# The opening of a four-layer graph network on one core: load order, copies, and three jobs moved to GpSimd

## The chip, the cores and the metric

The kernel runs on one NeuronCore of a Trainium2 chip. The core has five instruction streams: TensorE (PE, with PEld for its weight loads), VectorE (DVE), ScalarE (ACT), GpSimd (POOL) and SyncE (SP). DMAs are issued from the streams of SP, ACT and POOL. The metric is the device time of the whole program in microseconds: 1605.96 before the change, the median of three runs (1605.39 to 1606.01).

## What is computed

Input `x` holds 32 graphs of 512 nodes with 128 features, in float32; `adj` is one 512 x 512 adjacency matrix for all of them. Four layers follow one another, each on a normalised and clipped input, and each added to `x`:

```python
h = maximum(layernorm(x), 0)
# layer 0: attention over edges
x_h  = elu(h @ Wi + bi)
e    = sigmoid(a_tgt[:, :, None] + a_src[:, None, :] + be) * mask   # mask = adj + 0.005 * (adj == 0)
agg  = einsum('bij,bjh->bih', e, x_h)
self_part = x_h * sum(e, axis=-1, keepdims=True)
x += concat([elu(concat([agg, self_part]) @ Wn + bn), x_h]) @ Wm + bm
# layer 1: five gated steps, each with adj @ h, then three gates; x += h
# layer 2: x += adj @ (h @ weight) + bias
# layer 3: x += sum over k of (adj^k @ h) @ W_k, k = 0..3, each power twice
```

The attention layer's "sum of the scores" is the sum of `e` over neighbours; it and the mask matter below.

## The kernel before, in words

One core handles the 32 graphs in eight groups of four (`G = 4`). A feature matrix is a tile of 128 partitions by 512 columns; the adjacency is four such tiles, here called quarters. All large products are on TensorE.

The program isn't written in its final order. Each step is recorded with `op(engine, cost, due, emit, reads, writes)`, and a planner (`Plan.order`, L135) lays the steps out engine by engine: it replays the recorded costs, starts on each engine the ready step with the earliest due time, and gives out buffers. The resulting order is fixed when the program is built; each engine then runs its own list in order, and semaphores hold an instruction until its inputs are there. `plan.nudge` (L233) shifts the due times of some steps by random amounts drawn from a list of seeds (`HEAD_NUDGES`, L25), for steps due between 0 and 130; the order up to 250 is laid out with them.

Where PE has no ready step the planner may put in `plan.idle` (L347), a product of the constant `ones` with itself that nothing reads. These are called fillers here. They are allowed until 50 on the planner's clock (`FILL`), and one is placed unless another PE step becomes ready within `idle.us` = 0.224.

The program opens as follows.
- SP loads graph 0 (`load_graph`, L377), weights and the next graphs. ACT issues the four quarters of the adjacency (L361 through `load`, called at L386) and then, with a first tiny `tanh` (L355), loads its function table. A hardware DMA's landing is told by one of eight semaphores that are handed out in turn, in program order; a ninth DMA waits, on the engine that issues it, until the first user of its semaphore has landed.
- PE turns the quarters (L574); ACT writes rounded copies of the quarters as they came (`nat`, L583) and of the turned ones (`adj_rows`, L584). DVE counts the entries that are neither 0 nor 1 (L560), PE adds the counts up (L590), and every engine reads the result and branches (L1106). With a binary adjacency the program goes to the arm `binary = True`, which runs in the profile.
- In the arm, 16 products of `nat` and `adj_rows` make the square of the adjacency (L906), the mask is made from `adj_rows` on ACT (L828), and the first four graphs go through the attention layer. `scored` projects a graph (L490 with `Wi_sb`), takes the ELU on ACT and DVE (L603 to L615), makes messages and end scores (L643). `aggregated` makes the four score tiles `es` on ACT (L704), masks them on DVE (L707), multiplies them with the messages (L715) and sums them for `self_part`.
- That sum is made in three ways: for graphs 0 and 1 the four tiles are added in two pairs on DVE (L727) and each pair is multiplied with `ones` on PE; for graph 2 the four are added into one by three additions on DVE (L736), split into a high and a low rounded part (L747, L748) and multiplied with `ones_r` (L753); from graph 3 on the additions are accumulating DMAs (L743).
- Layer norms put a power of -0.5 on POOL (L527) between DVE's moments (L522 to L525) and its scaling (L542).

Of the kernel before, what the change touches and what calls it, by code (L numbers as in the profile page):

```python
# [21 lines left out]


HEAD, TAIL = 250.0, 1500.0
HEAD_NUDGES = (7100000, 7100078, 7100153, 7100154, 7100740, 7100413, 7100768, 7100794, 7100559, 7100664, 7100595,  # L25
    7100631, 7100754, 7100963, 7100652, 7100659, 7100662, 7100678, 7100697, 7100699, 7100706,
    7100965, 7100730, 7100733, 7100742, 7100786, 7100966, 7100797, 7100813, 7100877, 7100824,
    7100834, 7100860, 7100864, 7100866, 7100875, 7100881, 7100884, 7100901, 7100907, 7100908,
    7100911, 7100919, 7100920, 7100922, 7100934, 7100936, 7100941, 7100945, 7100946, 7100949,
    7100950, 7100955, 7100970, 7100973)  # L30
TAIL_NUDGES = ()


# [19 lines left out]
class Plan:  # L53
# [7 lines left out]
    def __init__(self, slots, ahead, last):  # L61
        self.ahead, self.last, self.ops, self.vals = ahead, last, [], {}
        self.free = {k: [(0.0, i) for i in range(n)] for k, n in slots.items()}
        self.until = dict.fromkeys(self.RESULT, 0.0)
        self.shared, self.now = 0.0, 0.0
        self.careful = 0.0
        self.slack = 0.0
        self.pieces = {}
        self.cold = 4.5
        self.fill = 0.0  # L70
        self.idle = None
        self.complete = False

    def op(self, eng, us, due, emit, reads=(), writes=(), two=None, keep=0, result=None,
# [60 lines left out]
    def order(self, end=None):  # L135
# [35 lines left out]
        while events:  # L171
# [3 lines left out]
            for e in self.until:  # L175
                while coming[e] and coming[e][0][0] <= now:
                    _, i, o = heapq.heappop(coming[e])
                    heapq.heappush(ready[e], (o.turn, i, o))
                if self.until[e] > now:
                    continue  # L180
                passed, o = [], None
                while ready[e] and o is None:
                    x = heapq.heappop(ready[e])
                    if begins(x[2], now):
                        o = x[2]
                    else:
                        passed.append(x)
                for x in passed:
                    heapq.heappush(ready[e], x)
                if o is not None and now < self.careful and any(  # L190
                    c.turn < o.turn and t < now + 0.3 * o.us for t, _, c in coming[e]
                ):
                    heapq.heappush(ready[e], (o.turn, index[o], o))
                    o = None
                if o is None and e == "PE" and self.idle.known <= now < self.fill and not (
                    coming[e] and coming[e][0][0] < now + self.idle.us):
                    order.append(self.idle)
                    self.until[e] = now + self.idle.us * (1.9 if now < self.cold else 1.0)
                    heapq.heappush(events, self.until[e])
                if o is None:  # L200
                    continue
                order.append(o)
                o.begun = True
                while oldest + 1 < len(by_turn) and by_turn[oldest].begun:
                    oldest += 1
                o.start, self.until[e] = now, now + o.us
                if o.two:
                    self.shared = self.until[e]
                for v in o.takes:
                    v.slot = self.free[v.kind].pop(self.clean(now) if v.added else 0)[1]  # L210
                    if v.kind == "b":
                        self.pieces[v.slot] = v.pieces
                o.known = self.until[e] + o.result
                heapq.heappush(events, self.until[e])
                heapq.heappush(events, o.known)
                for v in o.vals:
                    v.left -= 1
                    if not v.left and v.kind:
                        self.free[v.kind].append((o.known, v.slot))
                        self.free[v.kind].sort()  # L220
                for a in o.after:
                    if a in index:
                        a.waits -= 1
                        a.ready = max(a.ready, self.known(o, a))
                        if not a.waits:
                            heapq.heappush(coming[a.eng], (a.ready, index[a], a))
                            heapq.heappush(events, a.ready)
# [24 lines left out]
def tile_four_graph_layers(  # L252
# [37 lines left out]
    MARGIN = 10.0  # L290
    FIRST = 4
    ONES = 0
    SPLIT = False
    SQUARE, NAT = 12.0, 0.0
    BRANCHES = 0.75
    A_LANDS = (3.0, 3.3, 3.6, 3.8)

    T_MM, T_TR, T_NARROW, T_PASS = 0.86, 0.44, 0.224, 0.23
    T_VEC, T_COPY, T_ACT, T_DMA = 0.605, 0.5, 0.6, 0.45
# [2 lines left out]
    plan = Plan(slots, ahead=60.0, last=(B - 2) * PACE)  # L302
    op = plan.op
    plan.careful = 18.0

    cpool = ctx.enter_context(tc.tile_pool(name="const", bufs=1))
    pool = ctx.enter_context(tc.tile_pool(name="slots", bufs=1))
# [28 lines left out]
    def chunks(t):  # L336
# [2 lines left out]

    ident, ones, neg_half = const("ident", [P, P]), const("ones", [P, P]), const("nhalf", [P, NC])  # L340
    op("POOL", 1.0, -9, lambda: make_identity(nc, at(ident)), [], [ident])
    op("DVE", 0.2, -9, lambda: nc.vector.memset(at(ones), 1.0), [], [ones])


    spare = places["b"].pop()
# [6 lines left out]
    op("POOL", 0.4, 5, lambda: nc.gpsimd.tensor_copy(at(ones_r), at(ones)), [ones], [ones_r])  # L352

    warm = Val("s")
    op("ACT", 1.4, -9, lambda: nc.scalar.activation(  # L355
        at(warm)[:, :1], at(ones)[:, :1], AF.Tanh), [ones], [warm])


# [15 lines left out]
        v.left += 1  # L374
    plan.vals.update(dict.fromkeys([*X_group, *X]))

    def load_graph(b, due, result=None):  # L377
        op("SP", 0.48, due, lambda: nc.sync.dma_start(
            at(X[b]), x[b].rearrange("(p c) d -> p c d", c=NC)),
            [], [X_group[b // G], X[b]] if b % G == 0 else [X[b]], result=result)  # L380


    load_graph(0, -10, 2.5)
    A_nat = [Val("f") for _ in range(NC)]
    for ic, v in enumerate(A_nat):
        load(v, adj.rearrange("(p c) n -> c p n", c=NC)[ic], -9.5, 0.45, result=A_LANDS[ic], eng="ACT")  # L386
    Wi_sb = load_const(Wi, [P, P], "Wi_sb", -9)
    bi_sb = load_column(bi, "bi_sb", -9)
    load_graph(1, -8.5, 4.3)
    load_graph(2, -8, 4.5)  # L390


    W_tok = const("W_tok", [P, P + 2])
    load(W_tok, Wn[:P], -7, to=lambda t: t[:, :P], result=4.5)
    load(W_tok, We.rearrange("(t p) o -> p (t o)", p=P), -7, to=lambda t: t[:, P:])
    be_sb = load_const(be.partition_broadcast(P), [P, 1], "be_sb", -7, result=4.3)
    Wn_sb = load_const(Wn[P:], [P, P], "Wn_sb", -6, result=4.0)
    bn_sb = load_column(bn, "bn_sb", -6, result=3.6)
    Wm_sb = load_const(Wm.rearrange("(t p) o -> p t o", p=P), [P, 2, P], "Wm_sb", -5)
    bm_bc = load_const(bm.partition_broadcast(P), [P, P], "bm_bc", -5, earliest=BRANCH)  # L400
    load_graph(3, -6, 3.6)

# [177 lines left out]
    plan.vals.update(dict.fromkeys([adj_r, *adj_rows]))  # L580
    nat = [Val("q") for _ in range(NC)]
    for jc, pt in enumerate(adjacency_turned(-1)):
        op("ACT", T_COPY, NAT + jc, lambda jc=jc: nc.scalar.copy(chunks(at(nat[jc])), by_token(A_nat[jc])), [A_nat[jc]], [nat[jc]])  # L583
        op("ACT", T_COPY, jc, lambda jc=jc, pt=pt: nc.scalar.copy(at(adj_rows[jc]), at(pt)),  # L584
           [pt], [adj_rows[jc], adj_r])
    p_odd = Val("b")
# [38 lines left out]
    def scored(b, hT, due):  # L625
        KEEP = 12
        if b >= G:
# [1 line left out]
        pace = 0.6 if b < FIRST else 1.0  # L629
        d = due + 6 * pace  # L630
        xhT = elu(product(Wi_sb, hT, d, blocks=b >= G), bi_sb, bi_half, d, KEEP,
                  relu_by_vector=b < 2)

        d = due + 14 * pace
        msg, ends = Val("f"), Val("s")
# [58 lines left out]
    def aggregated(b, begun, due):  # L694
# [28 lines left out]
        elif b < 2:  # L723
            ps = Val("b")
            pair = [Val("f"), Val("f")]
            for i in range(2):
                op("DVE", T_VEC, d - 6, lambda i=i: nc.vector.tensor_tensor(  # L727
                    at(pair[i]), at(es[2 * i]), at(es[2 * i + 1]), op=ALU.add),
                    [es[2 * i], es[2 * i + 1]], [pair[i]], two=True)
            for i in range(2):  # L730
                product(ones, pair[i], d - 1, ps, start=i == 0, stop=i == 1)
        else:
            sums = [Val("f")]
            if b < 3:
                for n in range(1, NC):
                    op("DVE", T_VEC, d - 10, lambda n=n: nc.vector.tensor_tensor(  # L736
                        at(sums[0]), at(es[0] if n == 1 else sums[0]), at(es[n]), op=ALU.add),
                        [es[n], es[0] if n == 1 else sums[0]], [sums[0]], two=True)
            else:
                op("SP", T_DMA, d - 10, lambda: nc.sync.dma_start(at(sums[0]), at(es[0])),  # L740
                   [es[0]], [sums[0]], result=2.6)
# [76 lines left out]
    def list_rest(binary, pool):  # L818
# [6 lines left out]
            rows = [Val(tile=adjT.tile[:, jc, :]) for jc in range(NC)]  # L825
        for jc, pt in enumerate([None] * NC if binary else adjacency_turned(9)):
            def masked(jc=jc):
                nc.scalar.activation(at(mask)[:, jc, :], at(adj_rows[jc]).bitcast(F32), AF.Identity,  # L828
                                     bias=at(ones)[:, :1], scale=1 / ALPHA - 1)
            if binary:  # L830
                op("ACT", T_COPY, 9 + jc, masked, [adj_rows[jc], ones], [mask])
                continue
            z, row = Val("f"), rows[jc]
            op("ACT", T_COPY, 9 + jc, lambda z=z, pt=pt: nc.scalar.mul(at(z), at(pt), 1 / ALPHA), [pt], [z])
# [66 lines left out]
        if binary:  # L901
            adj2T = Val(tile=pool.tile([P, NC, N], F32R, tag="AA", name="AA"))
            squares = [Val("b") for _ in range(NC)]
            for n in range(NC * NC):
                kc, jc = divmod(n, NC) if SPLIT else divmod(n, NC)[::-1]
                op("PE", T_PASS, SQUARE, lambda jc=jc, kc=kc, pt=squares[jc]: nc.tensor.matmul(  # L906
                    at(pt), at(nat[kc])[:, ts(jc, P)], at(rows[kc]), start=kc == 0, stop=kc == NC - 1),
                    [nat[kc], rows[kc]], [squares[jc]])
            for jc, pt in enumerate(squares):
                op("ACT", T_COPY, SQUARE, lambda jc=jc, pt=pt: nc.scalar.copy(  # L910
# [240 lines left out]
```

## Time and profile before

One execution was profiled. It took 1605.48 us by the device's clock; the profile's own span is 1603.6 us.

| engine | busy us | share | instructions |
|---|---|---|---|
| PEld | 1024.3 | 64% | 6321 |
| DVE | 1404.7 | 88% | 3314 |
| ACT | 1130.4 | 70% | 2129 |
| POOL | 240.3 | 15% | 240 |

The opening, in groups of instructions:

| line | engine, step | count | ns of one (mean; L707: median) |
|---|---|---|---|
| L583 | ACT, rounded copy of a quarter | 4 | 1147 |
| L828 | ACT, mask | 4 | 714 |
| L707 | DVE, masking of a score tile | 16 in the first 60 us | 682 |
| L527 | POOL, power | 128 | 1231 |
| L894 | POOL, folding weights, 64 columns | 6 | 1404 |

Times in the views are microseconds from the span's start. A row of the timeline gives the start, the length, the engine, the line, the operation, what it writes and reads, and in brackets how long the engine was idle before and what ended that. In a row of the windows the stretch is followed by the busy time of PE, PEld, DVE, ACT and POOL (with counts), the granted TensorE clock (1.00 is full), the share of the DMA engines that is busy, and GB/s. A float32 product stands in the records as two matmuls. Matmuls are pipelined, so the distance from one start to the next is what one costs, and the recorded length is longer.

### The profile page before, as it was taken

To read this page: it belongs to the slowest core of one execution; us is meant where nothing else is said; L and a number is where in the kernel's file an instruction comes from. 1 tells how busy PE (TensorE), PEld (TensorE's weight loads), DVE (VectorE), ACT (ScalarE), POOL (GpSimd) and SP (SyncE) were. 2 spreads that over 40 slices of the span, in tenths; PEclk is the share of its full clock that TensorE was granted. 3 is DMA by queue.
4 is the path that set the end of the run, shared out by engine and by line. 5 is a ranking of instruction groups with operands and counts; after the bars stand their busy time and mean duration, and the time that the engine had idled before them with its cause. 6 is when DMAs were issued, how large, how long until landed. Compare 5 with 4: busy or idle time off the path is not lost.

```text
span 1603.6 us, 20898 instructions
## 1 busy us (share of the span) xinstructions
PE 1596.1 (100%) x6321; PEld 1024.3 (64%) x6321; DVE 1404.7 (88%) x3314; ACT 1130.4 (70%) x2129; POOL 240.3 (15%) x240
## 2 busy tenths in 40 slices
PE   9999999999999999999999999999999999999998
PEld 7655555666666666666666666666666666656687
DVE  8899989998988899989988899888998889878862
ACT  8877777877866767667766678676787677665661
POOL 2121101211111111211111111111111101100010
PEclk9999999999999999999999999999999999999999
DMA  3365335443543345544445534454444444333221
GB/s 109 80 152 145 112 111 140 121 130 106 144 126 115 105 126 136 137 122 111 121 125 145 126 96 128 119 148 119 132 130 124 125 120 129 90 91 99 86 60 49
DMA packets 272634, 188.01 MB, mean 117 GB/s; under 512 B 77312, under 2 KB 221568, under 8 KB 272512
## 3 DMA queue, kind: packets, MB, share of 16 engines
q1 hardware_dynamic: 257824, 161.93, 33.8%
q0 software_dynamic: 12528, 22.81, 8.5%
q10 hardware_dynamic: 2160, 1.84, 0.3%
q8 instruction: 52, 0.85, 0.2%
q14 instruction: 70, 0.57, 0.1%
HBM read 82.78 MB, written 73.33 MB: 97 GB/s over the span
## 4 chain that ended last, share of the span: by engine, by line
PE 99%; DMA 0%; DVE 0%; ACTq 0%; issue 0%
PE b L490 46%; PE b L950 26%; PE b L1025 7%; PE b L715 7%; PE b L1034 4%; PE b L766 4%; PE b L643 2%; PE b L1013 2%; PE b L753 1%; DMA f<-in_adj_dram 0%; PE b L419 0%; PE b L347 0%; PE b L906 0%; ACTq L361 0%; PE b L680 0%; DVE s L522 0%
## 5 line engine op out<-in xcount | busy, mean ns | idle before, releaser
L479 ACT COPY f<-b 128x512 f32<-128x512 f32 x388 | 223.7, 584 | 146.5 <-PE b L950 101.1
L950 PE MATMUL b<-AQ,r 128*128 128x512 f32 x1024 | 305.4, 440 | 0.0
L527 POOL TENSOR_TENSOR s<-s,nhalf 128x4 f32<-128x4 f32 x128 | 156.6, 1231 | 968.2 <-DVE s L525 774.6
L950 PEld LDWEIGHTS b<-AQ,r 128*128 128x128 f32 x1024 | 192.3, 188 | 90.8 <-issue 50.0
L975 DVE TENSOR_TENSOR f<-f,b 128x512 f32<-128x512 f32 x320 | 212.7, 676 | 24.5 <-PE b L490 18.5
L431 DVE STREAM_TRANSPOSE f<-f 128x512 f32<-128x512 f32 x246 | 207.3, 846 | 20.7 <-ACT f L536 19.7
L536 ACT ACTIVATE f<-x,s 128x128 f32<-128x128 f32 x496 | 203.8, 487 | 27.7 <-DVE s L531 27.3
L950 PE MATMUL b<-adj_r,r 128*128 128x512 f32 x768 | 220.8, 430 | 0.0
L495 ACT ACTIVATE f<-f,b4w 128x512 f32<-128x512 f32 x160 | 115.6, 723 | 116.8 <-DVE f L975 116.3
L950 PEld LDWEIGHTS b<-adj_r,r 128*128 128x128 f32 x768 | 143.8, 188 | 59.2 <-issue 27.3
L924 DVE TENSOR_TENSOR r<-f,r 128x512 fp32r<-128x512 f32 x224 | 152.5, 683 | 13.1 <-ACT r L920 12.7
L490 PE MATMUL b<-f,w4T 128*128 128x512 f32 x320 | 163.2, 592 | 0.0
L490 PE MATMUL b<-f,u3T 128*128 128x512 f32 x320 | 163.1, 592 | 0.0
L490 PE MATMUL b<-f,w5T 128*128 128x512 f32 x320 | 162.9, 592 | 0.0
L490 PE MATMUL b<-f,u5T 128*128 128x512 f32 x320 | 162.9, 592 | 0.0
L490 PE MATMUL b<-f,w3T 128*128 128x512 f32 x320 | 162.7, 592 | 0.0
L495 ACT ACTIVATE f<-b,b5w 128x512 f32<-128x512 f32 x160 | 109.2, 684 | 54.9 <-PE b L490 49.9
L920 ACT CAST r<-f 128x512 fp32r<-128x512 f32 x224 | 137.7, 619 | 12.3 <-DMA f<-m 11.9
L495 ACT ACTIVATE f<-f,b3w 128x512 f32<-128x512 f32 x160 | 115.0, 721 | 38.9 <-DVE f L975 38.4
L992 DVE TENSOR_TENSOR f<-f,f 128x512 f32<-128x512 f32 x160 | 109.2, 683 | 30.7 <-ACT f L495 30.3
L1025 PEld LDWEIGHTS b<-V,f 128*128 128x128 f32 x1024 | 122.7, 192 | 14.8 <-issue 12.7
L743 POOL DMA_DIRECT2D f<-f x87 | 78.8, 918 | 348.9 <-DVE f L975 54.6
(114 smaller groups left out, 2370.4 us busy)
## 6 DMA issues: line engine op xcount, KB each, us to landing
m<-f SPq DMA_DIRECT2D x246, 256.0 KB, 2.1
f<-m SPq DMA_DIRECT2D x186, 256.0 KB, 2.9
f<-f POOLq DMA_DIRECT2D x87, 256.0 KB, 3.8
f<-m SPq DMA_DIRECT2D x240, 64.0 KB, 2.4
x<-in_x_dram SPq DMA_DIRECT2D x32, 256.0 KB, 3.1
f<-f SPq DMA_DIRECT2D x29, 256.0 KB, 2.4
f<-d SPq DMA_DIRECT2D x28, 256.0 KB, 5.5
out_dram<-x SPq DMA_DIRECT2D x28, 256.0 KB, 2.4
```

The lines of the kernel that those rows point to most:

```text
L431: op("DVE", us, due, lambda: nc.vector.transpose(view_out(at(blocks)), view_in(at(src))), [src], [blocks])
L479: op("ACT", us, due, lambda: nc.scalar.copy(at(t), at(src)), [src], [t])
L490: nc.tensor.matmul(to, at(w), of, start=start, stop=stop)
L495: op("ACT", us, due, lambda: nc.scalar.activation(at(dst), at(src), AF.Tanh, bias=at(bias), scale=scale), [src, bias], [dst])
L527: op("POOL", 1.2, due, lambda: nc.gpsimd.tensor_tensor(stat(SCALE), stat(VAR), at(neg_half), op=ALU.pow), [s, neg_half], [s], two=False)
L536: nc.scalar.activation(at(h)[:, ts(c, P)], at(X[b])[:, c, :], AF.Relu, bias=stat(SHIFT)[:, c : c + 1], scale=stat(SCALE)[:, c : c + 1],)
L715: op("PE", T_MM, d, lambda jc=jc: nc.tensor.matmul(at(pn), at(msg)[:, ts(jc, P)], at(es[jc]), start=jc == 0, stop=False), [msg, es[jc]], [pn])
L920: op("ACT", T_COPY, due, lambda: nc.scalar.copy(part(hi), whole()), [src], [hi], keep=1)
L924: op("DVE", T_VEC, due, lambda: nc.vector.tensor_tensor(part(lo), whole(), part(hi).bitcast(F32), op=ALU.subtract), [src, hi], [lo], two=two)
L950: nc.tensor.matmul(at(pa), at(part)[:, ts(jc, P)], view(at(columns)[:, jc, :]), start=jc == n == 0, stop=jc == NC - 1 and n == PARTS - 1,)
L975: op("DVE", T_VEC, d, lambda: nc.vector.tensor_tensor(at(s), at(u), at(pg), op=ALU.add), [u, pg], [s])
L1025: nc.tensor.matmul(at(pz)[:, ts(i, D)], at(t[i])[:, ts(ic, P)], at(V[k]), start=i == n == 0, stop=last and i == G - 1 and n == len(terms) - 1,
```

## The change

- Table load first: the tiny `tanh` gets an earlier due time than the adjacency loads, so ACT loads its table and then issues the quarters, and the quarters' loads are not to be planned before 1.0.
- The loads behind graph 0 get `earliest` times for the planner: graph 1 not before 2.6, five weight loads not before 3.5; expected landings are changed. In the built order SP issues graph 0, Wi, bi, graph 2, graph 3, bn, graph 1, and then the other weights. The fourth quarter's semaphore is then the one of bi.
- `nat` is written with the same column order as the quarter, not regrouped by `by_token`; the squares read it through `by_token` instead.
- The squares' order by output is fixed, and their due time is 9 instead of 12.
- The mask moves from ACT to GpSimd.
- The sums of the scores of graphs 0, 1 and 2 (four pair additions and three additions) move from DVE to GpSimd.
- Graph 2's relu, in the first ELU, moves from ACT to DVE (`relu_by_vector=b < 3`).
- Until 10 on the planner's clock a filler is placed only where no other PE step becomes ready within 0.7 (0.224 before, and still behind 10).
- A new list of seeds; since costs, engines and due times change too, the planned order differs everywhere.

The built program has 20 fillers instead of 34 in the arm that runs: 10 before the branch and 10 behind it, where there were 17 and 17.

```diff
-HEAD_NUDGES = (7100000, 7100078, 7100153, 7100154, 7100740, 7100413, 7100768, 7100794, 7100559, 7100664, 7100595,
...
+HEAD_NUDGES = (7500046, 7500070, 15001300, 7500191, 7500223, 15000120, 15000078, 15000080, 15000672, 15000178,
...
+        self.unsure = 0.0
...
-                    coming[e] and coming[e][0][0] < now + self.idle.us):
+                    coming[e] and coming[e][0][0] < now + (self.idle.us if now > self.unsure else 0.7)):
...
-    SPLIT = False
-    SQUARE, NAT = 12.0, 0.0
+    ADD = 1.15
+    SQUARE, NAT = 9.0, 0.0
...
-    A_LANDS = (3.0, 3.3, 3.6, 3.8)
+    A_LANDS = (2.15, 2.4, 2.65, 2.9)
...
+    plan.unsure = 10.0
...
-    op("ACT", 1.4, -9, lambda: nc.scalar.activation(
+    op("ACT", 1.4, -9.9, lambda: nc.scalar.activation(
         at(warm)[:, :1], at(ones)[:, :1], AF.Tanh), [ones], [warm])
...
-    load_graph(0, -10, 2.5)
+    load_graph(0, -10, 2.45)
...
-        load(v, adj.rearrange("(p c) n -> c p n", c=NC)[ic], -9.5, 0.45, result=A_LANDS[ic], eng="ACT")
+        load(v, adj.rearrange("(p c) n -> c p n", c=NC)[ic], -9.5, 0.45, earliest=1.0, result=A_LANDS[ic], eng="ACT")
...
-    load_graph(1, -8.5, 4.3)
-    load_graph(2, -8, 4.5)
+    load_graph(1, -8.5, 3.7, 2.6)
+    load_graph(2, -8, 3.9)
...
-        op("ACT", T_COPY, NAT + jc, lambda jc=jc: nc.scalar.copy(chunks(at(nat[jc])), by_token(A_nat[jc])), [A_nat[jc]], [nat[jc]])
+        op("ACT", T_COPY, NAT + jc, lambda jc=jc: nc.scalar.copy(at(nat[jc]), at(A_nat[jc])), [A_nat[jc]], [nat[jc]])
...
-                  relu_by_vector=b < 2)
+                  relu_by_vector=b < 3)
...
-                op("DVE", T_VEC, d - 6, lambda i=i: nc.vector.tensor_tensor(
+                op("POOL", ADD, d - 6, lambda i=i: nc.gpsimd.tensor_tensor(
                     at(pair[i]), at(es[2 * i]), at(es[2 * i + 1]), op=ALU.add),
-                    [es[2 * i], es[2 * i + 1]], [pair[i]], two=True)
+                    [es[2 * i], es[2 * i + 1]], [pair[i]], two=False)
...
-                    op("DVE", T_VEC, d - 10, lambda n=n: nc.vector.tensor_tensor(
+                    op("POOL", ADD, d - 10, lambda n=n: nc.gpsimd.tensor_tensor(
                         at(sums[0]), at(es[0] if n == 1 else sums[0]), at(es[n]), op=ALU.add),
...
-                nc.scalar.activation(at(mask)[:, jc, :], at(adj_rows[jc]).bitcast(F32), AF.Identity,
-                                     bias=at(ones)[:, :1], scale=1 / ALPHA - 1)
+                nc.gpsimd.tensor_scalar(at(mask)[:, jc, :], at(adj_rows[jc]).bitcast(F32), 1 / ALPHA - 1, 1.0,
+                                        op0=ALU.mult, op1=ALU.add)
...
-                kc, jc = divmod(n, NC) if SPLIT else divmod(n, NC)[::-1]
+                jc, kc = divmod(n, NC)
...
-                    at(pt), at(nat[kc])[:, ts(jc, P)], at(rows[kc]), start=kc == 0, stop=kc == NC - 1),
+                    at(pt), by_token(nat[kc])[:, jc, :], at(rows[kc]), start=kc == 0, stop=kc == NC - 1),
```

## The prediction

> **What bounds the kernel now.** I read the busy table first, then the chain of waits, then the windows by stage.
>
> ```profile
> PE 1596.1 (100%) x6321; PEld 1024.3 (64%) x6321; DVE 1404.7 (88%) x3314; ACT 1130.4 (70%) x2129; POOL 240.3 (15%) x240
> ...
> PE 99%; DMA 0%; DVE 0%; ACTq 0%; issue 0%
> ```
> ```profile
> 5.00:10.00 5.00, 4.39 (x37) 4.00 (x37) 4.53 (x20) 5.00 (x6) 2.23 (x4) 1.00 0.97 301
> 11.27:23.60 12.33, 12.15 (x72) 9.53 (x70) 10.54 (x40) 12.14 (x25) 4.83 (x9) 1.00 0.43 114
> 23.60:35.00 11.40, 11.38 (x60) 7.59 (x60) 11.23 (x40) 9.36 (x21) 2.51 (x2) 1.00 0.06 24
> 35.00:1550.00 1515.00, 1515.00 (x5817) 955.29 (x5816) 1359.66 (x3156) 1085.33 (x2043) 226.07 (x214) 1.00 0.44 120
> ```
>
> PE carries the chain, and from 35 us on it has no gap in 1515 us. So the time is a sum on PE: the moment real products start, plus real products, plus fillers behind that moment, plus PE's stalls. The change leaves the real products alone: I counted 4229 matmuls without fillers in both programs' orders. Only the head can move the time. A reordered step after 35 us costs nothing unless it opens a gap, and I find no step there whose inputs come later.
>
> What the head consists of, from the chain, the timeline of PE and that of ACT:
>
> ```profile
> 2.14 5.67 DMA f<-in_adj_dram
> ...
> 7.86 0.75 PE b L574 x4
> 8.60 1.12 PE b L347 x10
> 9.72 0.27 PE b L590 x8
> ```
> ```profile
> 4.87 4.32 ACT L583 CAST q<-f 128x512 fp32r<-128x512 f32 x4 [0.74 <-DMA f<-in_adj_dram]
> ...
> 9.08 2.04 ACT L584 CAST adj_r<-b 128x512 fp32r<-128x512 f32 x4
> ```
> ```profile
> 11.27 0.94 PE L906 MATMUL b<-adj_r,q 128*128 128x512 f32 x3
> ```
> ```profile
> 22.14 1.28 PE L347 MATMUL b<-ones 128*128 128x128 f32 x10
> 23.60 0.67 PE L715 MATMUL b<-f,f 128*128 128x512 f32 x1 [0.18 <-DVE f L707]
> ```
>
> The last adjacency quarter lands at 2.14 + 5.67 = 7.81, and the first square (L906) starts at 11.27. Behind that stand 17 fillers of two records each (L347: 2, 6, 10, 2, 2, 6 and 6 records); ten records lie 0.112 apart, so one filler is 0.224 us and all are 3.8 us. PE's bare stalls there are about 0.7: 0.35 ahead of 23.60 and 0.36 among the next three products.
>
> **Part by part.**
>
> *Adjacency behind the table load.* ACT's four adjacency issues go from 0.73 to behind table load and warm-up (1.28 + 0.20), to about 2.05, 2.5 and 3.0 (0.47 apart) for the first three. The fourth is worse off. Eight landing semaphores are handed out in turn; before, the ninth load (third graph) starts at 4.86, just after the first quarter landed. In the new order the fourth quarter is a reused one and waits for the column bi. Queued behind that wait on ACT are the rounded copies, whose inputs land later anyway. bi stands behind x0 and Wi (320 KB); POOL could use it at 6.33 before, and without adjacency beside it I estimate 4.7 to 5.2. More important, SP now issues the third and fourth graphs at 2.1 and 2.6 and the second one beside that fourth quarter. Before, x0, Wi, x1 and four quarters (1600 KB) were in by 7.81; now two graphs more (512 KB) stand ahead. The 5 to 10 us window shows the DMA engines 97% busy, in its full slices near 370 GB/s, so 512 KB are 1.4 us. As the graphs use another queue and may finish after the quarter, I take two thirds: landing at **8.7**, range 8.0 to 9.4.
>
> *Contiguous copies, fewer early fillers.* The four copies take 4.32 us, ending 9.19, behind the landing by 1.4. Contiguous, one costs what L584 costs a step, about 0.48, and only the last one is left behind the landing. Ready then are: transposes 0.75, four casts 3 x 0.48 + 0.61 (last row landing + 2.84, but the first square needs only early rows); the count: DVE's last L560 0.69, L542 1.03, L595 0.15, then 0.73 from L595's end to PE's branch, as now (10.17 to 10.90), so landing + 2.65. Before, ten fillers (1.12) also stood in front of the count. First square at landing + 2.75 instead of + 3.46: 8.7 + 2.75 = **11.45, +0.2 us**. The squares now load weights with a stride, as L574 does: its load is 0.06 longer than L419's, hidden below a pass of 0.23.
>
> *Fillers.* After the branch the new order has 10 instead of 17: 7 x 0.224 = **-1.6 us**, if no idle takes their place. Real PE work ahead of the first graph's product L715 in the new order: 16 squares 3.73, three projections 2.57, two turns 0.87, three weights 0.33, four swaps 0.93, four half-products 1.79, one spread 0.43, together 10.65; with 2.24 of fillers from 11.45 that is 24.3. DVE, resuming at 12.3, has 10.7 of rows (three moments 1.26, two norms 1.03, the ELU steps 0.60 to 0.65, small ones) plus one masking of 0.60: 23.6 to 24. They meet, so little idle replaces the fillers.
>
> *Mask to GpSimd.* ACT loses 4 x 0.61. GpSimd's price isn't in the trace; nearest are L352 and L932, 0.29 and 0.40 for 128 columns. With 0.21 as the fixed part (smallest L868) that makes 0.53 to 0.97; 1.6 at most if nothing is fixed. At 1.0, with two powers (1.03) in between, the masks end near 17.5, at 1.6 near 20. The first masking is at 23: nothing, cover 3 us. The second power and the swap cast wait behind them, each with over 1 us to spare. *Third graph's relu on DVE*: DVE +0.65, in the sum above.
>
> *Score sums to GpSimd.* Seven additions of 0.60 leave DVE. On GpSimd: folds L894 of 64 columns follow each other by 0.34, so 512 columns cost at most 2.7. [...]
>
> [...] The row first, POOL then DVE:
>
> ```profile
> 17.41 0.23 POOL L871 TENSOR_SCALAR b4w<-b4w 128x1 f32<-128x1 f32 x1
> ...
> 22.19 0.74 POOL L871 TENSOR_SCALAR b3w<-b3w 128x1 f32<-128x1 f32 x1
> ```
> ```profile
> 22.17 0.68 DVE L615 SCALAR_TENSOR_TENSOR f<-f,f 128x512 f32<-128x512 f32 x1
> ```
>
> The same tiny operation took 0.23 alone and 0.74 when it met L615, ending just behind it. Powers take 1.03 alone and 1.40 there; a fold 0.69 and 1.50. [...] In the trace GpSimd loses 0.4 to 0.8, while DVE beside the folds loses at most 0.23 (L924 0.92 for 0.69). [...]
>
> Who waits? Third graph: three additions in series after its last masking, 5.2, then cast 0.6, subtraction 0.7 and handoffs 0.2: ready at +6.7. PE gets there at +5.5 (multiplication 0.75, Wn product 0.86, four products 3.43, half-product 0.44): a stall of 1.2. Second graph: two additions end 3.5 after its third masking plus 0.6 of delay and handoff, PE's cover is 3.9 (four and a half products): 0.2. First graph: cover over 1.5, nothing. So **+1.4 us** over today's 0.7.
>
> **Sum** against the profiled execution (1605.48; span 1603.6 and 1.9 around it): +0.2 - 1.6 + 1.4 = 0.0, so 1605.5; the shown median 1605.96 lies 0.5 above that run. What can be told from no change is 0.2%, 3.2 us.
>
> **Rivals.**
> - *Even* (0.50): the gain in fillers is given back to the GpSimd sums: 1605.5, own range 1604.6 to 1607.
> - *Sums are hidden* (0.25): [...] 0.2 - 1.6 + 0.2, 1604.3; with an early quarter (8.0) 1603.6. For it: POOL is 15% busy. Against: rows that wait for DVE.
> - *GpSimd sums become the bound* (0.20), on the other side: at 2.6 each, by strided folds or by waiting through bursts of four maskings (2.4), the third graph's are ready at 7.8 + 1.5 = 9.3, a stall of 3.8, the second's at 5.8 against 3.9, 1.9 more. A PE held by the second comes later to the third, so together 3.8 to 5.7, in the middle 4.8: 0.2 - 1.6 + 4.8 = +3.4, 1608.9. It is slower than before from about 1.75 per addition on. For it: DVE 11.2 of 11.4 busy in that window. Against: a fold waits for two instructions at most.
> - *The front doesn't move as told* (0.05): a quarter landing at 6.5, 2.2 earlier than taken, with hidden sums gives 1602.1; nothing in the DMA load speaks for it.
>
> The range, 1603.7 to 1609.0, leaves out the last case and the slower half of the third. Slower by over 0.2% (above 1608.7 from the own run, 1609.2 from the median): 0.16, most of the third case with what I overlooked in the new order. Faster: 0.04, as all fillers gone and an early quarter together are needed. Within: 0.80.
>
> **What would show it.** Right: the first square between 10.8 and 12.1; the last adjacency issue not before bi's landing; 10 fillers behind it; the additions at 1.3 to 2.0; a PE stall at L765 (ones_r product) before 50 us; no gap after 60. Wrong: additions at 2.5 and PE waiting for POOL in three places; a quarter past 9.5; gaps after 60 us, which would mean the new order itself starves PE.

## The result, and the profile after

The changed kernel took **1611.59 us** (median of ten runs, 1609.03 to 1612.75); the kernel before, measured beside it, 1605.97. The ratio is 1.0031, with a 95% interval of 1.0021 to 1.0041: 5.6 us slower, outside the predicted range of 1603.7 to 1609.0. The profiled execution took 1612.75 us (span 1611.0), 7.3 us over the one before; it is the longest of the ten.

The busy table and the chain of the page, after:

```profile
PE 1598.4 (99%) x6293; PEld 1023.6 (64%) x6293; DVE 1405.5 (87%) x3308; ACT 1126.1 (70%) x2124; POOL 252.6 (16%) x251
...
PE 93%; DVE 3%; DMA 1%; ACT 1%; POOL 0%; issue 0%; SPq 0%; POOLq 0%; DVEq 0%
```

PE's own share of the chain falls from 99% to 93%: there are stretches now in which PE waits for others. The same windows as before, and the chain of waits of the first 20 us in order of time (start, length, what), tell where:

```profile
5.00:10.00 5.00, 2.20 (x11) 1.51 (x9) 1.84 (x6) 1.76 (x3) 1.66 (x3) 1.00 0.80 268
11.27:23.60 12.33, 12.33 (x64) 10.46 (x63) 9.63 (x45) 7.46 (x16) 7.38 (x13) 0.77 0.33 91
23.60:35.00 11.40, 11.07 (x52) 6.62 (x50) 11.30 (x28) 10.14 (x22) 4.46 (x3) 1.00 0.01 1
35.00:1550.00 1515.00, 1512.22 (x5779) 950.25 (x5780) 1358.13 (x3153) 1082.24 (x2035) 233.51 (x219) 1.00 0.44 120
```
```profile
1.65 4.07 DMA bi_sb<-in_L_gnn_bi_dram
...
5.75 4.60 DMA f<-in_adj_dram
...
10.39 1.13 PE b L586 x4
```
```profile
13.87 3.27 PE L918 MATMUL b<-adj_r,q 128*128 128x512 f32 x7
```

- Eight loads were issued without a wait for a landing. The next three were each held by one: bn by graph 0, until 3.56, graph 1 by Wi, until 4.57, and the last adjacency quarter by bi, which landed at 5.72, until 5.75. The quarter was in at 10.35 instead of 7.81. In the 5 to 10 us window PE is busy 2.20 us instead of 4.39. The first square starts at 13.87, 2.6 later than before.
- In the second window PE looks full, but the granted clock is 0.77: seven squares take 3.11 us from 13.87 to the next product at 16.98, 0.444 each, where they had taken 0.233.
- Behind 35 us, 2.8 us of idle have appeared where there was none.

### The profile page after: what moved, and what is told of

The parts are those of the page before. It is cut to its first block, busy times and chain, and to the rows that moved or that the text cites. A ratio compares the mean times of both kernels' runs of the same rounds, so it can differ in the third digit from the quotient of the medians.

```text
span 1611.0 us, 20846 instructions
## 1 busy us (share of the span) xinstructions
PE 1598.4 (99%) x6293; PEld 1023.6 (64%) x6293; DVE 1405.5 (87%) x3308; ACT 1126.1 (70%) x2124; POOL 252.6 (16%) x251
## 4 chain that ended last, share of the span: by engine, by line
PE 93%; DVE 3%; DMA 1%; ACT 1%; POOL 0%; issue 0%; SPq 0%; POOLq 0%; DVEq 0%
PE b L502 44%; PE b L962 25%; PE b L1037 7%; PE b L727 5%; PE b L1046 4%; PE b L778 3%; PE b L1025 2%; PE b L655 2%; DVE f L719 1%; PE b L765 1%; DMA m<-f 1%; DVE f L443 0%; PE b L918 0%; DMA f<-m 0%; POOL f L748 0%
## 5 line engine op out<-in xcount | busy, mean ns | idle before, releaser
L502 PE MATMUL b<-f,u3T 128*128 128x512 f32 x320 | 163.2, 592 | 0.5 <-DMA f<-m 0.5
L502 PE MATMUL b<-f,w4T 128*128 128x512 f32 x320 | 163.2, 592 | 0.2 <-ACT f L491 0.2
L502 PE MATMUL b<-f,w3T 128*128 128x512 f32 x320 | 163.2, 592 | 0.0
L502 PE MATMUL b<-f,u5T 128*128 128x512 f32 x320 | 162.8, 593 | 0.2 <-DVE f L994 0.2
L502 PE MATMUL b<-f,w5T 128*128 128x512 f32 x320 | 162.8, 592 | 0.0
```

The lines of the kernel that those rows point to most:

```text
L502: nc.tensor.matmul(to, at(w), of, start=start, stop=stop)
```

## Experiments

Seventeen runs. The third column is the median less that of the kernel before, measured beside the run; the interval is that of the ratio to it. Half of an interval is 1.0 to 2.2 us, so single steps of one microsecond are hints and not proofs.

| label | median us | minus before | ratio, interval |
|---|---|---|---|
| f1_more_fillers | 1612.98 | +7.4 | 1.0046 (1.0032 to 1.0060) |
| q1_quarter_first | 1610.31 | +4.8 | 1.0031 (1.0019 to 1.0042) |
| s1_sums_on_dve | 1610.90 | +5.3 | 1.0028 (1.0018 to 1.0039) |
| b1_no_late_fillers | 1605.70 | +0.1 | 1.0000 (0.9992 to 1.0008) |
| t1_loads_new_order | 1609.43 | +3.7 | 1.0022 (1.0013 to 1.0031) |
| g1_sums_on_pool | 1607.09 | +1.3 | 1.0006 (0.9998 to 1.0014) |
| q2_adj_before_table | 1607.77 | +2.0 | 1.0011 (1.0002 to 1.0019) |
| c1_contiguous | 1606.20 | +0.4 | 1.0002 (0.9994 to 1.0010) |
| q3_adj_first_sums_dve | 1608.16 | +2.7 | 1.0016 (1.0009 to 1.0022) |
| m1_mask_on_pool | 1605.33 | -0.1 | 0.9999 (0.9991 to 1.0007) |
| k1_relu_on_act | 1605.74 | +0.3 | 1.0002 (0.9993 to 1.0010) |
| o1_order_only | 1607.71 | +1.6 | 1.0008 (1.0000 to 1.0017) |
| r1_third_relu_on_act | 1607.35 | +1.2 | 1.0005 (0.9997 to 1.0013) |
| t2_loads_and_sums | 1611.63 | +5.5 | 1.0032 (1.0020 to 1.0045) |
| r2_third_relu_on_dve | 1607.68 | +1.5 | 1.0008 (0.9999 to 1.0016) |
| w1_bi_before_Wi | 1612.60 | +6.3 | 1.0036 (1.0022 to 1.0049) |
| w2_adj_first_relu_act | 1607.56 | +1.3 | 1.0005 (0.9996 to 1.0013) |

In all of them the plan is kept; only the list that it gave is permuted, fillers are put in or left out, or an engine or a column order is exchanged where an instruction is emitted, so that no other step changes its place.

### Is it the clock? f1_more_fillers

My first theory: PE idles where the early fillers had been, loses its clock, and the squares at half speed are the loss.

```diff
-    issue(plan.order(end=BRANCH))
+    first = plan.order(end=BRANCH)
+    turns = [n for n, o in enumerate(first) if o.emit.__name__ == "turn"]
+    sums = [n for n, o in enumerate(first) if o.emit.__name__ == "count"]
+    for n, more in ((sums[0], 2), (turns[3], 6), (turns[2], 6)):
+        first[n:n] = [plan.idle] * more
+    issue(first)
```

> The changed kernel with 14 more fillers on TensorE: 6 ahead of the third quarter's turn, 6 ahead of the fourth's, 2 ahead of the count; nothing else moves, the fourth quarter still lands near 10.4. Clock theory (TensorE idle from 6.5 to 8.1 and from 8.8 to 10.4 us cost it the granted clock, and squares at 0.47 instead of 0.23 us are the loss): granted clock at least 0.9 from 11 to 18 us, squares at 0.23, first square near 12.9 instead of 13.87, and 2 to 3 us less than the changed kernel, 1608.6 to 1609.6. Rival (VectorE sets the head's end, so a faster TensorE only waits more): the squares are fast again, but the time is within 0.7 us of the changed kernel's 1611.6.

PE and DVE of this run, on the timeline, and PE of q1_quarter_first, which turned out to be the changed kernel itself, executed once more (see below):

```profile
12.84 2.02 PE L923 MATMUL b<-adj_r,q 128*128 128x512 f32 x7
...
37.24 1.12 PE L502 MATMUL b<-f,Wn_sb 128*128 128x512 f32 x2 [1.47 <-DVE f L768]
```
```profile
18.12 0.87 DVE L534 BATCH_NORM_STATS2 s<-x 128x6 f32<-128x128 f32 x4 [1.53 <-DMA x<-in_x_dram]
```
```profile
16.00 1.02 PE L502 MATMUL b<-f,Wi_sb 128*128 128x512 f32 x2
...
37.27 1.12 PE L502 MATMUL b<-f,Wn_sb 128*128 128x512 f32 x2 [1.47 <-DVE f L768]
```

The first square comes at 12.84, the squares have their old speed, and the median is no lower. DVE's first row behind its branch starts at 13.89, as late as in the changed kernel (13.98), and DVE then waits 1.53 us for a graph that SP only asks for behind its own branch, at 13.43. A faster PE meets a late DVE sooner and idles (2.74 us between 11.27 and 60, 2.08 in the changed kernel). So the clock is not the main loss. It is not free either. In the profile of the changed kernel the product behind the seven squares starts at 16.98 and the one with `Wn_sb` at 38.27. In q1 the clock was back at 1.00 by 15 us: the first of these starts at 16.00, the second at 37.27, and f1, whose clock is 1.00 throughout, has the second at 37.24. Squares at half speed thus cost an execution about 1.0 us; full speed all along gains nothing beyond that.

### Is it the late quarter? q2_adj_before_table, t1_loads_new_order

Undone in the changed kernel:

```diff
+    first = plan.order(end=BRANCH)
+    loads = [o for o in first if o.eng == "ACT" and o.us == 0.45]
+    for o in loads:
+        first.remove(o)
+    n = next(n for n, o in enumerate(first) if o.eng == "ACT")
+    first[n:n] = loads
+    issue(first)
```

> The changed kernel with ScalarE's four adjacency issues ahead of its table load again, so that none of them is held for a landing; nothing else moves. Landing theory: quarter 4 lands at 7.8 to 8.6 instead of 10.37, VectorE is through its branch by 12.2, the first square comes before 12, 1.5 to 2.5 us less than the changed kernel, 1609 to 1610. Rival (the loss comes from what follows 20 us): quarter as early, time within 0.7 us of the changed kernel's 1611.4. If TensorE's clock is down all the same, it counts for nothing as long as VectorE is what TensorE waits for.

Done alone in the kernel before (graphs 1, 2 and 3 stand here where the changed kernel has 2, 3 and 1; places, sizes and semaphores are the same):

```diff
...
+    loads = [o for o in first if o.eng == "ACT" and o.us == 0.45]
+    graphs = [X[b].writer for b in (2, 3)]
+    column = bn_sb.writer
+    moved = [ones.writer, warmed, loads[0], graphs[0], loads[1], loads[2], column, graphs[1], loads[3]]
...
+    first[n + 1 : n + 1] = moved[2:]
+    issue(moved[:2] + first)
```

> The kernel before with one part of the change, the order of the first loads: ScalarE's table load and warm-up ahead of the four quarters, SyncE's third and fourth graph and bn ahead of the weights, so that the fourth quarter waits for the landing of bi as in the changed kernel. Landing theory (a late fourth quarter delays count, branch and VectorE, which is full until 40 us): quarter 4 lands at 10 to 10.7 us instead of 7.81, VectorE is through its branch near 13.9 instead of 11.96, and the time is 1.5 to 2.5 us above before, 1607.1 to 1608.1. Rival (the front has slack, the loss comes later): quarter as late, time within 0.6 us of before's 1605.6.

First PE of q2, then PE and DVE of t1:

```profile
7.71 0.75 PE L586 MATMUL b<-ident,f 128*128 128x128 f32 x4 [0.52 <-DMA f<-in_adj_dram]
...
10.93 2.04 PE L924 MATMUL b<-adj_r,q 128*128 128x512 f32 x7
...
34.72 1.13 PE L502 MATMUL b<-f,Wn_sb 128*128 128x512 f32 x2 [1.47 <-DVE f L768]
```
```profile
10.23 1.13 PE L574 MATMUL b<-ident,f 128*128 128x128 f32 x4 [1.11 <-DMA f<-in_adj_dram]
11.15 2.34 PE L347 MATMUL b<-ones 128*128 128x128 f32 x10
13.42 0.34 PE L590 MATMUL b<-ones,n_odd 128*1 128x1 f32 x8
```
```profile
13.80 0.14 DVE L595 CAST other<-b 1x1 int32<-1x1 f32 x1 [1.86 <-PE b L590]
```

With the quarters issued first, the last one lands at 7.66, the first square starts at 10.93 with full clock, and 3.6 us of the 5.6 are gone (+2.0 against before; its interval does not meet the one of the changed kernel). In the rows the product with `Wn_sb` starts at 34.72 instead of 38.27. Of these 3.55 us, 1.0 is the slow squares that the late quarter brought; the other 2.5 are gained over f1 as well (37.24), whose quarter is as late and whose PE is at full speed. The reverse costs +3.7 on its own, more than expected, and the rows show why: PE is at half speed (four turns in 1.13, 0.75 in q2), so the five fillers (ten records) ahead of the count take 2.27 us instead of 1.12, and DVE waits for the count. So in the old list the fillers, harmless at full speed, stand in the way, and 1.15 of the +3.7 are theirs. The late quarter, with the slow PE that comes with it, is the largest part of the loss, seen from both sides.

### Hold or bytes? q1_quarter_first, w1_bi_before_Wi

```diff
+    third_graph = [o for o in first if o.eng == "SP" and X[2] in o.vals]
...
+    n = first.index(loads[2]) + 1
+    first[n:n] = [loads[3], *third_graph]
```

> The changed kernel with the fourth adjacency quarter listed right behind the third and the third graph behind it, so that the quarter has a landing semaphore of its own and is not held until bi has landed. Landing theory: the quarter lands at 7.8 to 8.5 instead of 10.37, first square near 11.4, TensorE has no idle stretch over 1.2 us and keeps its clock, 3.5 to 5 us less than the changed kernel, 1606.6 to 1608.1. Rival (the clock is lost anyway, since the early fillers are still missing): landing as early, but granted clock under 0.8 between 9 and 14 us, squares at 0.35 to 0.47, only 1 to 2.5 us less. Second rival (VectorE decides): under 1 us less.

This edit was empty: `third_graph` found nothing, and the quarter's new place in the list, ahead of other engines' loads, left it waiting for bi as before. Every engine's instructions and waits came out as in the changed kernel. The run is a second measurement of it, +4.8 us.

```diff
+    first = plan.order(end=BRANCH)
+    a, b = first.index(Wi_sb.writer), first.index(bi_sb.writer)
+    first[a], first[b] = first[b], first[a]
+    issue(first)
```

> The changed kernel with the loads of bi and Wi exchanged on SyncE, so that the fourth quarter is held for the landing of Wi, which was in 1.2 us ahead of bi; the same bytes stand ahead of it. If the hold sets the landing: its issue moves from 5.75 to about 4.7 and the landing from 10.37 by as much, to 9.2 to 9.6, and the time by about 1 us, 1610 to 1611. If the bytes of the two graphs ahead of it set the landing: the issue moves, the landing stays within 0.4 us of 10.37, and the time within 0.6 us of 1611.5.

Neither, as the issue was not earlier: Wi in bi's place landed at 6.21, and the fourth quarter was issued at 6.24. But over the seven profiles with this order of loads (after, f1, q1, s1, t1, t2, w1) the issue goes from 5.75 to 7.10 and the landing only from 10.09 to 10.57, with no relation between them (5.75 to 10.35, 6.24 to 10.09, 7.10 to 10.31). So the hold puts the quarter behind all other early loads, and within this span of 1.35 us the moment of issue does not set the landing. That the bytes ahead of it do is only half of an answer. The changed kernel's windows:

```profile
8.50:9.00 0.50, 0.32 (x3) 0.13 (x2) 0.26 (x2) 0.18 (x1) 0.00 (x0) 1.00 0.70 268
9.00:9.25 0.25, 0.00 (x0) 0.00 (x0) 0.00 (x0) 0.00 (x0) 0.20 (x1) 1.00 0.17 51
```

The DMA engines are busy up to about 9 us; from there to 10.25 their share is 0.17 to 0.49, and the quarter lands at 10.35 all the same. What it waits for in this last stretch, and how far each of the other loads delays it, is open.

### Do GpSimd and VectorE shut each other out? s1_sums_on_dve, g1_sums_on_pool, q3_adj_first_sums_dve

In the changed kernel, POOL and DVE beside each other:

```profile
28.28 1.78 POOL L739 TENSOR_TENSOR f<-f,f 128x512 f32<-128x512 f32 x1 [0.38 <-DVE f L719]
30.69 1.27 POOL L739 TENSOR_TENSOR f<-f,f 128x512 f32<-128x512 f32 x1 [0.63 <-DVE f L719]
```
```profile
28.26 2.36 DVE L719 SCALAR_TENSOR_TENSOR f<-f,mask 128x512 f32<-128x512 f32 x2
...
30.67 2.14 DVE L554 TENSOR_SCALAR f<-x,s 128x128 f32<-128x128 f32 x4
...
36.33 1.29 DVE L719 SCALAR_TENSOR_TENSOR f<-f,mask 128x512 f32<-128x512 f32 x2
...
40.60 1.20 DVE L543 SCALAR_TENSOR_TENSOR s<-s 128x4 f32<-128x4 f32 x1
```
```profile
38.27 1.12 PE L502 MATMUL b<-f,Wn_sb 128*128 128x512 f32 x2 [1.47 <-DVE f L768]
```

Two maskings take 1.29 when POOL is quiet (36.33) and 2.36 when an addition runs (28.26); four scalings take 2.14, where they take 1.11 alone; a step on four columns 1.20 for 0.15. The addition itself takes 1.27 at its shortest and 1.78 behind a masking that began just before it (28.26, 28.28). So each holds up the other: 1.07, 1.03 and 1.05 on DVE's side, 0.51 on POOL's. These three rows alone cost DVE 3.2 us, of the 4.2 that seven additions of 0.60 had taken from it. PE waits 1.47 for the sum that DVE writes late (L768). Of the 13 maskings up to 60 us one is long, 1.76; the others take about 0.68 each.

With the additions back on DVE, by replacing `nc.gpsimd` with `nc.vector` where they are emitted:

> The changed kernel with the seven additions of the first three graphs' score sums on VectorE, at the places of the list where GpSimd had them; nothing else moves. Exclusion theory (a GpSimd addition and a masking shut each other out, which made maskings 1.1 to 1.6 us each and took some 4 us from VectorE): maskings back to 0.6 to 0.65, TensorE's gap at the Wn product near 38 us gone, 1.5 to 2.5 us less than the changed kernel, 1609 to 1610. Rival (VectorE is full either way: 7 x 0.60 = 4.2 us of additions come back to it in place of the waits): within 0.8 us of 1611.6, or up to 2 us more.

The kernel before with the two replaced the other way:

> The kernel before with another part alone: the seven additions of the first three graphs' score sums on GpSimd, listed where VectorE had them. Exclusion theory (an addition on GpSimd and a masking or an ELU step on VectorE shut each other out): maskings of 1.1 to 1.6 us beside additions of 1.3 to 2.8, TensorE gaps of 1.5 to 3 us in 25 to 50 us, time 1 to 2.5 us above before, 1606.6 to 1608.1. Rival (4.2 us less on a full VectorE is worth more than the waits): 0.5 to 1.5 us below before, 1604.1 to 1605.1.

DVE and POOL of g1:

```profile
35.34 3.57 DVE L707 SCALAR_TENSOR_TENSOR f<-f,mask 128x512 f32<-128x512 f32 x4
...
39.43 2.63 DVE L707 SCALAR_TENSOR_TENSOR f<-f,mask 128x512 f32<-128x512 f32 x3
```
```profile
36.70 1.66 POOL L727 TENSOR_TENSOR f<-f,f 128x512 f32<-128x512 f32 x1 [4.14 <-DVE f L707]
...
41.61 3.26 POOL L736 TENSOR_TENSOR f<-f,f 128x512 f32<-128x512 f32 x2 [1.29 <-PE b L490]
```

The same again: seven maskings of 0.62 grow by 1.8 us. As to time, s1 gains too little to tell (+5.3 against +5.6 and +4.8 for the changed kernel): PE's wait for L768 falls from 1.5 to 1.0, but one of 0.6 appears at another product (L692). g1's +1.3 has an interval that holds no change; among PE's waits, though, there is one for an addition on GpSimd, which the kernel before does not have:

```profile
PE b L490 <- POOL f L727: 0.6, 1, 0.6
```

Undone together with the late quarter:

> The changed kernel with both suspects undone at once: ScalarE's four adjacency issues ahead of its table load, and the seven additions of the score sums on VectorE. Two-part theory (late quarter some 3.5 us, exclusion between GpSimd and VectorE some 1.5 us, and nothing else costs): 1605.9 to 1606.9, within 1 us of before, and 0.8 to 1.8 us less than with the adjacency alone put back. Rival (mask, third relu or the new order of the head cost as well): 1607.5 or more, with TensorE gaps that wait for neither an addition nor the adjacency.

The sums bring nothing back here: 2.7 above before, and with them on GpSimd it was 2.0. So the rows show that the two hold each other up; how, they do not tell. In the new list DVE gets back in waits about what it was relieved of, and a loss in time does not show; in the old list a loss of about 1 us is likely, but it lies within the noise. The two-part theory falls too: a rest is left.

### The parts that were hidden: b1, c1, m1, k1

Before, without the ten fillers from the first turn to the branch:

```diff
+    first = plan.order(end=BRANCH)
+    n = [n for n, o in enumerate(first) if o.emit.__name__ == "turn"][0]
+    issue(first[:n] + [o for o in first[n:] if o is not plan.idle])
```

> The kernel before without the fillers between the first turn of the adjacency and the branch (ten of them); nothing else moves. Clock theory: TensorE idles 1.2 us twice between 8 and 11 us, the granted clock falls below 0.9 from 10 to 15 us, the squares behind the branch take 0.3 to 0.47 us each, and the time is 1 to 3 us more than before, 1607 to 1609. Rival (these fillers only fill waits): the clock stays at 1.0 and the first square comes up to 0.4 us earlier, 1605.4 to 1606.1.

The first square comes at 10.43 instead of 11.27, the clock stays, the time is the same. Idle times of at most 0.7 left PE at full speed (four turns in 0.75, at 7.88). DVE came through its branch 0.5 earlier; of the 0.8 us at the front 0.64 are left at 48 us (L753 at 48.23 instead of 48.87), which the medians do not show.

Before, with `nat` copied contiguously and the squares reading by token:

> The kernel before with the contiguous rounded copies alone (and the squares' strided weights). Copies at 0.62 instead of 1.15 us, the rows' casts end about 0.5 us earlier, the first square 0.2 to 0.4 us earlier; time 0 to 0.4 us below before, 1605.2 to 1605.6, since the ten fillers ahead of the count and the branch still stand. Rival (weights with a stride slow the squares): squares at 0.25 to 0.3 instead of 0.233, time up to 0.8 us above before.

Copies 0.62 each, the first square at 11.05, no change that can be told. Before, with `masked` on GpSimd as in the change:

> The kernel before with the mask's four rows on GpSimd alone, listed where ScalarE had them. Hidden (as step 4 of the prediction has it): rows of 0.6 us, time within 0.5 us of before's 1605.8. Rival (they keep VectorE or the powers of the normalizations waiting): 0.6 to 1.5 us above before.

No change. Before, with both of these and the first two graphs' relu emitted as an activation:

> The kernel before with the contiguous copies, the mask on GpSimd, and the relu of the first two graphs on ScalarE instead of VectorE (2 x 0.65 us off VectorE between 12 and 40 us). If VectorE alone sets where the head ends: 0.6 to 1.3 us below before, 1604.5 to 1605.2, with fewer TensorE gaps ahead of 35 us. Rival (ScalarE, 12.1 of 12.3 us busy there before, or TensorE's own fixed list takes over): between 0.4 us below and 1 us above before.

No change either: ScalarE's relief does not buy a shorter head by this exchange. No version tried beats the kernel before.

### The rest: r2, r1, o1, w2, t2

Graph 2's relu, on VectorE in the kernel before:

```diff
+            op("ACT", T_ACT, due, lambda: nc.vector.tensor_scalar(
+                at(r), at(p), at(bias), 0.0, op0=ALU.add, op1=ALU.max)
+                if third else nc.scalar.activation(
...
```

> The kernel before with the third graph's relu on VectorE alone. VectorE full (0.65 us more on it): 0.3 to 0.8 us above before, 1605.9 to 1606.5. Rival (hidden): within 0.2 us of before.

Back on ScalarE in q3, and in q2:

> The kernel with adjacency first and sums on VectorE (1608.2), and the third graph's relu on ScalarE as well. Relu theory (0.65 us on a full VectorE): 0.4 to 0.9 us less, 1607.3 to 1607.8. Order theory: within 0.3 us of 1608.2.

> The changed kernel with two parts undone: adjacency issues ahead of the table load, third graph's relu on ScalarE. Sums and mask stay on GpSimd, copies contiguous. If relu and sums on VectorE's side are what is left: 1606.0 to 1607.0, 0.8 to 1.5 us less than with the adjacency alone put back, level with before or 1 us above. Rival (the GpSimd additions hold as much up as the relu does): 1607.2 to 1608.2.

PE's waits over 0.2 us from 10 to 60 us, in r2 and before (what waited, for what: sum, times, longest):

```profile
PE b L717 <- DVE f L709: 0.9, 2, 0.7
```
```profile
PE b L715 <- DVE f L707: 0.2, 1, 0.2
```

Three pairs agree in sign, each taken as a difference to its own measurement of the kernel before: r2 +1.5 over before, r1 1.5 below q3 (the medians themselves are 0.8 apart), w2 0.7 below q2. None is beyond its own interval; all three together make it likely that the relu costs about a microsecond: PE waits longer for the maskings queued behind it. Between w2 and r1 only the sums differ, and they are level (+1.3, +1.2).

Now every moved piece of work undone (as r1, and mask on ScalarE, copies by token), only the new list and its fillers left:

> The changed kernel with every moved piece of work back where it was: adjacency ahead of the table load, sums and nothing else of theirs on VectorE, mask and third graph's relu on ScalarE, strided copies. What is left of the change is the order of the list on each engine (new seeds, new cost figures) and the sparser fillers. Order theory (the list itself is 2 to 3 us worse on the chip): 1607.5 to 1608.7. Rival (the rest of the loss is the work that VectorE was given, or the strided weights): 1605.4 to 1606.4.

+1.6, with an interval that begins at 1.0000: the new list is likely a microsecond or more worse by itself, and r1 and w2 point the same way. The list includes SP's new order of loads, which no run put back. One step stands out in the rows. In all ten profiles with the new list DVE waits 0.6 to 1.5 us for the first graph that SP asks for behind its branch; in none of the nine with the old list does it. The changed kernel's row:

```profile
17.65 0.87 DVE L534 BATCH_NORM_STATS2 s<-x 128x6 f32<-128x128 f32 x4 [0.96 <-DMA x<-in_x_dram]
```

No run took this wait away, so what it costs is not shown. And two parts together in the old list:

> The kernel before with two parts of the change, the new order of the first loads and the sums on GpSimd. If their costs add up (3.7 and 1.3 us above before alone): 1610.2 to 1611.2, nearly all of the changed kernel's loss. Rival (behind a late front the exclusion falls into waits that are there anyway): 1608.8 to 1609.8.

+5.5 for 3.7 and 1.3: the two add up within the error, and are as much as the whole change loses. With the relu and the list the parts come to more than that, so they do not simply add: the late quarter is worth 3.6 in the new list and 3.7 in the old one, the sums about nothing in the new list and 1.3 in the old one. Why the sums differ is not shown.

## Why the prediction was wrong

- **Landing, 8.7 (8.0 to 9.4): the step that failed.** That the fourth quarter waits for bi was right, and bi landed at 5.72 (estimate 4.7 to 5.2). The forecast delay was 0.9 us, 7.81 to 8.7; the measured one is 2.5. The term for the bytes was too small: I let two thirds of two graphs pass ahead. In fact the quarter came behind everything SP had asked for, three graphs and a weight, which landed at 8.22, 8.80, 9.53 and 9.72. It landed at 10.35. The bytes are not all of it: the whole 576 KB more than before, at the prediction's 370 GB/s, make 1.6 us and 9.4 (an estimate). For the rest, in which the DMA engines are little busy, the working had no term, and its cause is open. My own sign of error, "a quarter past 9.5", appeared. The three first issues were not late at all: ACT's queue gave them out during the table load.

```profile
0.72 1.28 ACT L367 ACT_TABLE_LOAD   x1 [0.72 <-PEq L1149]
1.03 1.35 ACTq L373 DMA_DIRECT2D f<-in_adj_dram  x3
```

- **First square, landing + 2.75.** With PE at full speed it was +2.59 (f1), in the changed kernel +3.5, at half clock. That fewer fillers beside a late quarter could cost the clock was missing from my working; the profile shown loses about 1.0 us to it, q1 nothing. First square: 11.45 predicted, 13.87 found.
- **Fillers, -1.6 "if no idle takes their place".** Idle took it: between 11.27 and 60 us PE idles 2.08 us instead of 0.20. In b1, too, ten fillers fewer ahead of the branch buy nothing that the medians show. Where DVE is late, a filler stands in a wait that is there anyway; my -1.6 counted it as a cost.
- **Sums, +1.4.** The additions are 1.27 to 1.79. What I took for one, three in 5.2, the trace before does not show. Its rows give about the same (an estimate): a fold's 0.34 for 64 columns, 0.21 of it taken as fixed, makes 1.25 for 512, and the 0.4 that POOL lost beside DVE makes that 1.65, three in 5.0. PE's stall, though, is not at L765, where it waits 0.5 at the weight load. It stands where DVE is held up (L502, 1.47). I took it that DVE loses at most 0.23, as beside the folds; beside the additions it loses over 1.0 in each of three rows. In time the new list shows no loss from it (s1, q3).
- **Mask.** 0.60 to 0.63 each, in my bounds, hidden (m1).
- **Third relu.** I put +0.65 into DVE's sum and said that DVE and PE "meet". On an engine that is nearly full (11.23 of 11.40 us from 23.60 on, before) 0.65 more pushes back what follows: it likely costs about 1 us.
- **"A reordered step after 35 us costs nothing unless it opens a gap, and I find no step there whose inputs come later."** Gaps came. After 60 us PE idles 1.03 us in the profile of the changed kernel and 0.12 in that of q1, the same program:

```profile
60.00:200.00 140.00, 139.29 (x475) 1.00 0.48 130
200.00:1550.00 1350.00, 1349.68 (x5200) 1.00 0.44 120
```
```profile
60.00:200.00 140.00, 139.99 (x479) 1.00 0.48 132
200.00:1550.00 1350.00, 1349.89 (x5221) 1.00 0.44 120
```

The two executions are 3.1 us apart (1612.75 and 1609.61): 1.0 is the clock in the head, 0.9 are these gaps, the rest is open. In the ten profiles with the new list PE idles 0.03 to 1.18 us between 60 and 1550, in the nine with the old list 0 to 0.28. The spread of the runs does not show it: the kernel before stayed within 2.1 us in the ten runs beside the changed kernel (3.7), but within 4.8 us in 34 others.

My cases held the loss in "sums become the bound" at 0.20. The sign of that case came, its mechanism did not: the largest part was a load.

Left open: the list's own share (1.2 to 1.6, at the edge of what was measured), whether DVE's wait for a late graph is its cause, what opens the late gaps, and what delays the quarter beyond the bytes.

## What to carry to other kernels

Before a load is moved, follow its semaphore and everything that will stand ahead of it; it may be held until another has landed and then come in last (here until 5.72, and in at 10.35). Where a second engine is as late as the bound, removing fillers or idle from the bound may buy little (b1: +0.1 us for ten fillers fewer), and work put on the second engine can show in full (r2: likely about 1 us for 0.65). Undo each part alone in both kernels: a bundle of parts that each look hidden can carry one that is not.

## What was not expected of the hardware

- Ten filler records took 2.27 us in t1 (11.15 to 13.42) and 1.12 before, while the granted clock stands at 1.00 there. In the changed kernel the same half speed is shown as 0.50. So the column alone does not tell whether PE is at half speed; the distance of equal records does.
- In the changed kernel the third quarter's turns ran at full speed (0.75 for four, at 8.08); after 1.57 us of idle the fourth's ran at half (1.13, at 10.39). That one idle time is not the reason: 1.62 us of idle ahead of 8.08 had left it at full speed. PE was little busy in the whole stretch, 2.20 of 5 us. In b1 idle times up to 0.7 us left it at full speed. Once at half speed it stayed so for 6.6 us of nearly full work (10.39 to 16.98); in q1 full speed was back by 15 us. What sets off the fall, and what ends it, these runs do not tell.
